# Layer 0 of a four-layer kernel, from units of 512 tokens to one pipeline of 128-token chunks

## The chip, the cores and the metric

The kernel runs on one core of a Trainium2 chip. A core has five engines with queues of their own: TensorE (PE in the profile, with its weight loads as PEld), VectorE (DVE), ScalarE (ACT), GpSimd (POOL) and SyncE (SP), which here issues the transfers. The metric is the device time of one execution in microseconds, and the time of a kernel is the median of its runs.

## The reference

The input x has 16 images of 192 channels and 32 x 32 pixels in float32. Four layers follow one another; only the first, an mLSTM block with a convolution, is touched. Ahead of it every image is group-normalised. Cut to what matters (S is 1024 tokens, INNER 384, 12 heads of 32):

```python
h = layernorm(seq)
x_in, z = split(h @ w_up + b_up)
x_act = silu(causal_conv4(x_in))
q, k, v = x_act @ w_q, x_act @ w_k, x_in
i_pre, f_pre = concat(q, k, v) @ w_i + b_i, concat(q, k, v) @ w_f + b_f
# scan over the tokens, for each head:
m_new = max(log_sigmoid(f) + m, i)
C_new = f_s * C + i_s * outer(v, k * 32 ** -0.5)
n_new = f_s * n + i_s * k * 32 ** -0.5
h = (C_new @ q) / max(abs(n_new @ q), 1)
# after the scan:
hn = (h - mean(h)) / sqrt(var(h) + 1e-5) * mh_w + mh_b      # per token and head
x1 = seq + ((hn + skip * x_act) * silu(z)) @ w_down + b_down
y = conv3x3(x1 + silu(seq @ w_lin + b_lin)) + conv2_b
y = leaky_relu(batchnorm(y))                                  # statistics over all images
```

Layers 1 to 3 (a Mamba block, a depthwise convolution with batch norm, a block with four scan directions) are the same in both kernels.

## The kernel before

Layer 0 works on 32 units, two for each image, of 512 tokens (U). Each unit has two parts, written as Python generators that yield between steps.

The front (`layer0_front`) loads and normalises the image (for the first unit of an image), applies the layer norm, the up projection (L452, evicted to xin at L454 and to sz at L456), the causal convolution on DVE (L460, L464), the x_lin projection (L472, L475), three silu passes on ACT (L479) between two loads of activation tables (the second is L481), q and k (L490, evicted at L494 and L496), and the gates. The gate part leaves three things: u and w, on 12 partitions, and a row in DRAM.

The back (`layer0_back`) turns the scan over tokens into four chunks of 128. `layer0_decays` transposes u and w. `layer0_weigh` reads the row back to all partitions as e (128 x 12 x 128), adds the causal mask (L576) and u (L577) on POOL and takes the exponential on ACT (L578). `layer0_chunk` does a chunk: scores of k and q (L654), transposes of k (L660, copied to kt at L661) and of xin (L664, copied to v at L667), p as scores times e on DVE (L671), the part from the carried state, it (L676), the part from the chunk, num (L681), their sum h, the division by the denominator (L693 to L696), and the new state (L702 to L713).

Once all four chunks stand in hs, the head norm takes the whole unit at once: mean (L601), subtraction (L603), square (L605), variance (L607), the power -0.5 on POOL (L610 takes its result; the power itself is recorded at the helper's line L240), then the transposes to channels first (L617), scale and bias on ACT (L621), skip on DVE (L624), gate on POOL (L625), and the down projection (L632, L635) into a padded image ypad. The 3 x 3 convolution of an image (`layer0_conv2`, L408, four parts of 18 matmuls) reads it once both of its units are there.

What sets the order: the program is traced in Python, and the framework's scheduler then lays each engine's queue out in the order in which, by its own times, instructions become ready, earlier traced ones first. At run time each queue goes in that order, with semaphore waits. The class `Side` spreads the front of unit i + 1 and the two convolution parts of the image before over the steps of unit i's back.

PSUM has eight banks here: two named mm, which take most results and the convolution's accumulation over half a unit, four for the scores (s), one for it and one for num. Most SBUF tiles have two buffers.

A float32 matmul shows as two records in the profile, a transpose as one.

Of the kernel before, what the change touches and what calls it, by code (L numbers as in the profile page):

```python
# [19 lines left out]
HP = 96  # L20
DI = 384
S = 1024
W = 32
# [172 lines left out]

class Unit:
# [8 lines left out]
class Program:  # L206
# [113 lines left out]
    def layer0(self):  # L320
        tc = self.tc
        with (
            tc.tile_pool(name="w0", bufs=1) as wp,
            tc.tile_pool(name="s0", bufs=2) as sp,
            tc.tile_pool(name="b0", bufs=2) as bp,
            tc.tile_pool(name="d0", bufs=3, space=DRAM) as dp,
            tc.tile_pool(name="ps0", bufs=2, space=PSUM) as psum,
        ):
            self.layer0_weights(wp, bp, psum)
            self.stats = wp.tile([HP, 2, 2 * self.nb, 6], F32, name="stats")  # L330
            n = self.nb * S // U
            self.unit = {}
            self.image = {}
            finish(self.layer0_front(0, sp, bp, dp, psum))
            side, yields = Side(), 20
            for i in range(n):
                b, u = divmod(i, S // U)
                if i + 1 < n:
                    side.add("front", self.layer0_front(i + 1, sp, bp, dp, psum), i, i + 0.95)
                if b > 0:  # L340
                    for j in range(2):
                        side.add("conv", self.layer0_conv2(b - 1, 2 * u + j, bp, psum), i + 0.5 * j, i + 0.5 * j + 0.5)
                done = 0
                for _ in self.layer0_back(i, sp, bp, psum):
                    done += 1
                    side.tick(i + min(done / yields, 1.0))
                yields = done
                side.tick(i + 1)
            for u in range(4):
                finish(self.layer0_conv2(self.nb - 1, u, bp, psum))  # L350
            self.batch_norm(sp, "0bn_g", "0bn_b", self.bn0)
# [47 lines left out]
    def layer0_conv2(self, b, part, bp, psum):  # L399
# [4 lines left out]
        ps = psum.tile([128, 512], F32, name="mm")  # L404
# [14 lines left out]
    def layer0_front(self, i, sp, bp, dp, psum):  # L419
# [64 lines left out]
        unit = {"xin": xin, "sz": sz, "xact": xact, "xl": xl}  # L484
        for w, name, scale in ((self.w_q, "q", 1.0), (self.w_k, "k", DH**-0.5)):
# [12 lines left out]
            if name == "q":  # L498
                yield from self.layer0_gates(unit, carry, sp, dp, psum)
        self.unit[i] = unit  # L500
# [70 lines left out]
    def layer0_weigh(self, c, unit, bp):  # L571

        nc = self.nc
        e = bp.tile([128, NH, 128], F32, name="e")
        nc.sync.dma_start(e, unit["row"][:, c * 128 : (c + 1) * 128].partition_broadcast(128))
        nc.gpsimd.tensor_tensor(e, e, self.k0("mask")[:, None, :].to_broadcast([128, NH, 128]), ADD)  # L576
        nc.gpsimd.tensor_tensor(e, e, unit["uw"][:, c, 0][:, :, None].to_broadcast([128, NH, 128]), ADD)  # L577
        nc.scalar.activation(e, e, AF.Exp)  # L578
        return e

    def layer0_back(self, i, sp, bp, psum):

        nc = self.nc
        b, u = divmod(i, S // U)
        unit = self.unit[i]
        xact, sz, xl = unit["xact"], unit["sz"], unit["xl"]
        state = None if u == 0 else self.unit.pop(i - 1)["state"]
        self.layer0_decays(unit, sp, psum)
        yield
        hs = bp.tile([128, NCH, NH, DH], F32, name="hs", bufs=1)  # L590
        e = [self.layer0_weigh(0, unit, bp)]
        for c in range(NCH):
            if c + 1 < NCH:
                e.append(self.layer0_weigh(c + 1, unit, bp))
            state = yield from self.layer0_chunk(u * NCH + c, c, unit, e[c], state, hs, sp, bp, psum)
        unit["state"] = state

        hv = hs.rearrange("p c h d -> p (c h) d")
        n = NCH * NH
        mean = sp.tile([128, n], F32, name="mhm")  # L600
        nc.vector.tensor_reduce(mean, hv, AX.X, ADD)  # L601
        nc.vector.tensor_scalar(mean, mean, 1.0 / DH, None, MUL)
        nc.gpsimd.tensor_tensor(hv, hv, mean[:, :, None].to_broadcast([128, n, DH]), SUB)  # L603
        sq = bp.tile([128, NH, 128], F32, name="e").rearrange("p h (c d) -> p (h c) d", d=DH)
        nc.scalar.activation(sq, hv, AF.Square)  # L605
        var = sp.tile([128, n], F32, name="mhv")
        nc.vector.tensor_reduce(var, sq, AX.X, ADD)  # L607
        nc.vector.tensor_scalar(var, var, 1.0 / DH, EPS, MUL, ADD)
        self.pow_mhalf(var)
        nc.gpsimd.tensor_tensor(hv, hv, var[:, :, None].to_broadcast([128, n, DH]), MUL)  # L610
        yield

        ht = bp.tile([128, 3, U], F32, name="ht", bufs=1)
        for t in range(3):
            ps = psum.tile([128, 512], F32, name="mm")
            for c in range(NCH):
                nc.tensor.transpose(  # L617
                    ps[:, c * 128 : (c + 1) * 128],
                    hs[:, c, 4 * t : 4 * t + 4].rearrange("p h d -> p (h d)"), self.k("ident"),
                )  # L620
            nc.scalar.activation(  # L621
                ht[:, t], ps, AF.Identity, bias=self.v128("0mh_b", t), scale=self.v128("0mh_w", t)
            )
            nc.vector.scalar_tensor_tensor(ht[:, t], xact[:, t], self.v128("0skip", t), ht[:, t], MUL, ADD)  # L624
            nc.gpsimd.tensor_tensor(ht[:, t], ht[:, t], sz[:, t], MUL)  # L625
            yield
        yp = self.ypad[b % 2]
        rows = U // W
        for m in range(2):
            ps = psum.tile([128, 512], F32, name="mm")  # L630
            for k in range(3):
                nc.tensor.matmul(  # L632
                    ps[:HP], self.w_down[:, k, m * HP : (m + 1) * HP], ht[:, k], start=k == 0, stop=k == 2
# [4 lines left out]
                xl[:, m].rearrange("p (a b) -> p a b", b=W), ADD, ADD,  # L638
            )
            yield  # L640

    def layer0_chunk(self, n, c, g, e, state, hs, sp, bp, psum):

        nc = self.nc
        q, k_, xin = g["q"], g["k"], g["xin"]
        ch = slice(c * 128, (c + 1) * 128)
        v1 = self.v1[n % 2]
        ev = e.rearrange("p (i j) t -> p j i t", j=4)

        ss = [psum.tile([128, 3, 128], F32, name="s", bufs=4) for _ in range(4)]  # L650
        for i in range(3):
            for j in range(4):
                part = slice(32 * j, 32 * j + 32)
                nc.tensor.matmul(ss[j][:, i], k_[part, i, ch], q[part, i, ch], start=True, stop=True)  # L654
        yield

        kt = bp.tile([128, DI], F32, name="kt")
        ps = psum.tile([128, 512], F32, name="mm")
        for t in range(3):
            nc.tensor.transpose(ps[:, t * 128 : (t + 1) * 128], k_[:, t, ch], self.k("ident"))  # L660
        nc.scalar.copy(kt, ps[:, :DI])  # L661
        ps = psum.tile([128, 512], F32, name="mm")
        for t in range(3):
            nc.tensor.transpose(  # L664
                ps[:, t * 128 : (t + 1) * 128], xin[:, t, 3 + c * 128 : 3 + (c + 1) * 128], self.k("ident")
            )
        nc.scalar.copy(v1[:, :, :DH], ps[:, :DI].rearrange("p (h d) -> p h d", h=NH))  # L667
        p = []
        for j in range(4):
            p.append(bp.tile([128, 3, 128], F32, name="p", bufs=3))  # L670
            nc.vector.tensor_tensor(p[j], ss[j], ev[:, j], MUL)  # L671
        yield
        if state is not None:
            it = psum.tile([128, 512], F32, name="it", bufs=1)
            for i in range(3):
                nc.tensor.matmul(it[:, i * 132 : (i + 1) * 132], q[:, i, ch], state[:, i], start=True, stop=True)  # L676
        yield
        num = psum.tile([128, NH, DH + 1], F32, name="num", bufs=1)
        for j in range(4):
            for i in range(3):  # L680
                nc.tensor.matmul(num[:, 4 * i + j], p[j][:, i], v1[:, 4 * i + j], start=True, stop=True)  # L681
        yield
        h = bp.tile([128, NH, DH + 1], F32, name="h")
        if state is None:
            nc.vector.tensor_copy(h, num)
        else:
            nc.vector.tensor_tensor(
                h, it[:, :396].rearrange("p (h d) -> p h d", h=NH),
                g["uw"][:, c, 1][:, :, None].to_broadcast([128, NH, DH + 1]), MUL,
            )  # L690
            nc.vector.tensor_tensor(h, h, num, ADD)
        den = sp.tile([128, NH], F32, name="den")
        nc.vector.scalar_tensor_tensor(den, h[:, :, DH], -1.0, h[:, :, DH], MUL, MAX)  # L693
        nc.vector.tensor_scalar(den, den, 1.0, None, MAX)
        nc.vector.reciprocal(den, den)  # L695
        nc.gpsimd.tensor_tensor(hs[:, c], h[:, :, :DH], den[:, :, None].to_broadcast([128, NH, DH]), MUL)  # L696

        vr = bp.tile([128, NH, DH + 1], F32, name="vr")
        nc.gpsimd.tensor_tensor(vr, v1, e[:, :, 127][:, :, None].to_broadcast([128, NH, DH + 1]), MUL)  # L699
# [780 lines left out]
```

## Time and profile before

The kernel takes 19,994.89 us, the median of three runs from 19,978.39 to 20,020.1. The profiled execution has a span of 20,007.8 us.

| engine | busy, us | share of the span | share from 80 to 4740 us |
|---|---|---|---|
| PE | 17,439.3 | 87% | 3,628.10 of 4,660 (78%) |
| DVE | 13,103.0 | 65% | 1,817.57 (39%) |
| ACT | 12,711.5 | 64% | 1,084.05 (23%) |
| POOL | 12,611.8 | 63% | 1,695.59 (36%) |

The last column is layer 0's stretch. The page's second part cuts the span into 40 slices of about 500 us and gives the busy share of each in tenths; the row PEclk gives the TensorE clock that was granted, in tenths of full speed. A group of instructions is listed with its line, engine, operation, the tiles it writes and reads, its count, its busy time and the mean of one, and the idle time of the engine before it with what ended it. Line numbers are those of the kernel before.

### The profile page before, as it was taken

The page shows a single profiled execution, that of the slowest core. Times are in us where ns is not written, and L with a number is a line of the kernel's source. Part 1 is how long each engine was busy: PE and PEld are TensorE (multiplying, and loading weights), DVE is VectorE, ACT ScalarE, POOL GpSimd, SP SyncE. Part 2 cuts the span into 40 slices and gives each one's busy share as a digit, 9 for nine tenths or more (in the row PEclk, how much of TensorE's full clock was granted, in tenths as well). Part 3 has the DMA queues.
Part 4 walks back from the last instruction along what each step waited for, and adds up shares of the span by engine and source line. Part 5 has one row for each costly group of instructions (what it writes and reads, how often), then busy time and mean ns, then how long its engine had stood idle before and what let it go on. Part 6 is the DMA issues. An engine that isn't in the chain of part 4 may idle for free. (4 is left out here: it accounts for less than half of the span.)

```text
span 20007.8 us, 251373 instructions
## 1 busy us (share of the span) xinstructions
PE 17439.3 (87%) x92796; PEld 11473.9 (57%) x92796; DVE 13103.0 (65%) x14590; ACT 12711.5 (64%) x21185; POOL 12611.8 (63%) x6105
## 2 busy tenths in 40 slices
PE   7777777777999999978899999989998999999898
PEld 3343334434555555546666666666666666666666
DVE  3333343333777777747677877777787778777778
ACT  2222222223666666638778887888788788878888
POOL 3333333333555555537677877787787778877878
PEclk8888888888999999989999999999999999999999
DMA  1111111111222222212222222222222222222222
GB/s 40 25 27 30 27 27 29 26 26 39 62 60 61 61 61 61 60 59 64 74 70 77 75 74 71 77 72 74 73 77 73 70 77 77 73 71 77 72 72 65
DMA packets 713002, 1194.70 MB, mean 60 GB/s; under 512 B 60733, under 2 KB 300062, under 8 KB 699390
## 3 DMA queue, kind: packets, MB, share of 16 engines
q1 hardware_dynamic: 711774, 1178.62, 20.0%
q8 instruction: 735, 12.04, 0.2%
q14 instruction: 493, 4.04, 0.1%
HBM read 1030.13 MB, written 148.25 MB: 59 GB/s over the span
## 5 line engine op out<-in xcount | busy, mean ns | idle before, releaser
L847 POOL TENSOR_TENSOR h<-h,cb 128x1536 f32<-128x1536 f32 x2560 | 8848.5, 3460 | 1207.3 <-DVE h L840 1033.3
L821 ACT ACTIVATE da<-dt,neg_a 128x512 f32<-128x512 f32 x7680 | 5170.6, 714 | 1575.9 <-DVE h L840 1503.7
L828 PE MATMUL xb<-const,xbt 128*128 128x128 f32 x30720 | 5139.3, 283 | 506.4 <-ACT xbt L812 249.7
L840 DVE TENSOR_TENSOR_SCAN h<-da,carry,xb 128x512 f32<-128x512 f32 x3840 | 4663.4, 1263 | 1202.8 <-PE xb L828 923.4
L812 ACT ACTIVATE xbt<-ut,bt 128x384 f32<-128x384 f32 x8960 | 4880.2, 605 | 579.7 <-PE xb L828 572.0
L840 DVE TENSOR_TENSOR_SCAN h<-da,xb 128x512 f32<-128x512 f32 x3840 | 4442.0, 1202 | 1147.0 <-PE xb L828 851.3
L828 PEld LDWEIGHTS xb<-const,xbt 128*128 128x128 f32 x30720 | 3782.9, 145 | 2121.7 <-issue 866.1
L858 PE MATMUL y<-const,h 128*128 128x128 f32 x30720 | 4796.9, 280 | 66.5 <-POOL h L847 33.7
L858 PEld LDWEIGHTS y<-const,h 128*128 128x128 f32 x30720 | 3737.7, 145 | 231.6 <-issue 68.3
L810 POOL TENSOR_SCALAR xbt<-ut,bt 128x384 f32<-128x384 f32 x1280 | 1595.9, 1247 | 1476.4 <-PE xb L828 1074.8
L1401 PE MATMUL mm<-xin,dconv 128*128 128x512 f32 x3072 | 1461.3, 620 | 188.7 <-DMA dconv<-d_conv 187.6
L408 PE MATMUL mm<-ypad,w_conv 96*96 96x512 f32 x2304 | 1196.4, 638 | 11.8 <-ACT kt L661 6.3
L846 POOL COPY carry<-h 128x3 f32<-128x3 f32 x1280 | 245.9, 192 | 1424.0 <-DVE h L840 1321.6
L1401 PEld LDWEIGHTS mm<-xin,dconv 128*128 128x128 f32 x3072 | 576.7, 197 | 831.6 <-issue 632.4
L696 POOL TENSOR_TENSOR hs<-h,den 128x384 f32<-128x384 f32 x128 | 107.5, 840 | 1108.4 <-DVE den L695 1108.4
L578 ACT ACTIVATE e<-e 128x1536 f32<-128x1536 f32 x128 | 189.8, 1483 | 931.4 <-POOL e L577 913.0
L738 PE MATMUL mm<-xc,w_x 128*44 128x512 f32 x960 | 654.3, 800 | 54.9 <-ACT xc L1072 54.5
L757 PE MATMUL mm<-dbl,w_dt 65*128 65x512 f32 x960 | 525.6, 633 | 119.7 <-DVE dt L762 86.3
L408 PEld LDWEIGHTS mm<-ypad,w_conv 96*96 96x96 f32 x2304 | 370.4, 175 | 439.2 <-issue 412.1
L699 POOL TENSOR_TENSOR vr<-v,e 128x396 f32<-128x396 f32 x128 | 122.9, 960 | 791.6 <-ACT v L667 791.6
L1163 PE MATMUL mm<-xpad,d_dw 96*96 96x512 f32 x1152 | 587.5, 649 | 38.6 <-DVE xpad L1143 38.6
L1163 PE MATMUL mm<-xpad,dconv 96*96 96x512 f32 x1152 | 569.3, 633 | 54.9 <-DMA dconv<-d_dw 41.6
(272 smaller groups left out, 18918.4 us busy)
## 6 DMA issues: line engine op xcount, KB each, us to landing
cb<-row SPq DMA_DIRECT2D x2560, 256.0 KB
e<-row SPq DMA_DIRECT2D x128, 768.0 KB
dconv<-d_conv SPq DMA_DIRECT2D x144, 512.0 KB
x<-x SPq DMA_DIRECT2D x48, 768.0 KB
sz<-tmp SPq DMA_DIRECT2D x32, 768.0 KB
xrows<-xtok SPq DMA_DIRECT2D x32, 768.0 KB
xtok<-xrows SPq DMA_DIRECT2D x128, 192.0 KB
tmp<-sz SPq DMA_DIRECT2D x32, 768.0 KB
```

Source lines behind the costliest of these rows:

```text
L408: nc.tensor.matmul(ps[:HP], self.w_c2[:, k, t, m * HP : (m + 1) * HP], yp[:, k, r0 : r0 + 16, t % 3 : t % 3 + W], start=t + k == 0, stop=t ...
L738: nc.tensor.matmul(ps[:XD], w_x[t], seen[:, t], start=t == 0, stop=t == 2)
L757: nc.tensor.matmul(ps, w_dt[:, t * 128 : (t + 1) * 128], dbl, start=True, stop=True)
L810: nc.gpsimd.tensor_scalar(t[:, c], u.ut[:, c], b, None, MUL)
L812: nc.scalar.activation(t[:, c], u.ut[:, c], AF.Copy, scale=b)
L821: nc.scalar.activation(da[i, t], u.dt[:, t], AF.Exp, scale=u.neg_a(t, n))
L828: in_order(nc.tensor.transpose(xb[i, t][:, c * 128 : (c + 1) * 128], xbt[i][:, c, t * 128 : (t + 1) * 128], ident))
L840: nc.vector.tensor_tensor_scan(hv, dv, xv, 0.0 if first else u.carry_in[:, n, t : t + 1], MUL, ADD)
L847: nc.gpsimd.tensor_tensor(h[i], h[i], u.c.pop(n)[:, None, :].to_broadcast([128, 3, 512]), MUL)
L858: in_order(nc.tensor.matmul(u.y[:, j], h[i][:, t, c * 128 : (c + 1) * 128], ident, is_transpose=True, start=n == 0 and j % 4 == 0, stop=n ...
L1163: self.nc.tensor.matmul(ps, diags[t], pad[:, r0 : r0 + 16, c0 : c0 + W], start=t == 0, stop=t == n - 1)
L1401: nc.tensor.matmul(ps, dc[:, j], xin[:, r0 : r0 + 16, j % 4 : j % 4 + W], start=n == 0 and j == 0, stop=n == 1 and j == 7,)
```

## The change

In the changed kernel layer 0 has no backs. One loop goes over all 128 chunks of all images (`for g in range(n + 2)`), and each step does parts of four chunks: the down projection of chunk g - 2 if it is the last of its unit, p, h and the state of chunk g, weights and scores of chunk g + 1, the transposes, gate and skip of chunk g - 1, and the head norm of chunk g. Fronts and convolution parts are spread over the steps by fixed times. The purpose is that the chain of norm, gate and down projection never stands between two units with nothing beside it.

The norm is now per chunk, without the division: with d = max(n q, 1 in absolute value), (h/d - mean) / sqrt(var + eps) is (h - mean h) / sqrt(var h + eps d^2), where h is undivided. The power -0.5 is exp(-0.5 ln(.)) on ACT. Bias, skip, weight and gate are folded at the end of the front: xs = (skip x_act + mh_b) silu(z) and sw = mh_w silu(z), so that a chunk needs one product and one sum. kt is copied on DVE instead of ACT. The convolution accumulates in a PSUM bank of its own, and it goes to the mm pair.

```diff
+            for i in range(1, self.nb * S // U):
+                side.add("front", self.layer0_front(i, sp, bp, dp, psum), NCH * i - 3.9, NCH * i - 1.2)
+            for b in range(self.nb - 1):
+                for j in range(4):
+                    at = 8 * b + 9.2 + 1.9 * j
+                    side.add("conv", self.layer0_conv2(b, j, bp, psum), at, at + 1.9)
...
+            for g in range(n + 2):
+                for j, _ in enumerate(self.layer0_step(g, n, chunks, sp, bp, psum)):
+                    side.tick(g + j / 8)
...
-        ps = psum.tile([128, 512], F32, name="mm")
+        ps = psum.tile([128, 512], F32, name="conv", bufs=1)
...
+        for t in range(3):
+            nc.scalar.activation(
+                xact[:, t], xact[:, t], AF.Identity, bias=self.v128("0mh_b", t), scale=self.v128("0skip", t)
+            )
+        nc.gpsimd.tensor_tensor(xact, xact, sz, MUL)
+        yield
+        for t in range(3):
+            nc.scalar.activation(sz[:, t], sz[:, t], AF.Copy, scale=self.v128("0mh_w", t))
+        unit |= {"xs": xact, "sw": sz}
...
-        nc.scalar.copy(kt, ps[:, :DI])
+        nc.vector.tensor_copy(k.kt, ps[:, :DI])
...
-            it = psum.tile([128, 512], F32, name="it", bufs=1)
+                it = psum.tile([128, 512], F32, name="mm")
...
+    def layer0_step(self, g, n, chunks, sp, bp, psum):
+        k, new = chunks.get(g), None
+        last = chunks.pop(g - 2, None)
+        if last and last.c == NCH - 1:
+            self.layer0_down(last.unit, psum)
+        yield
+        if k:
...
+            yield
...
+            yield
+            self.layer0_state(k, vr, chunks.get(g - 1) if g % (S // 128) else None, bp, psum)
+            yield
+        if new:
+            yield from self.layer0_scores(new, bp, psum)
+        if g - 1 in chunks:
+            self.layer0_output(chunks[g - 1], bp, psum)
+            yield
+        if k:
+            self.layer0_norm(k, h, sp, bp)
+            yield
...
+    def layer0_norm(self, k, h, sp, bp):
+        nc.vector.tensor_reduce(mean, x, AX.X, ADD)
+        nc.vector.tensor_scalar(mean, mean, 1.0 / DH, None, MUL)
+        nc.gpsimd.tensor_tensor(hs, x, mean[:, :, None].to_broadcast([128, NH, DH]), SUB)
+        nc.scalar.activation(sq, hs, AF.Square)
+        nc.vector.tensor_tensor(d, h[:, :, DH], h[:, :, DH], MUL)
+        nc.vector.tensor_scalar(d, d, 1.0, EPS, MAX, MUL)
+        nc.vector.tensor_reduce(var, sq, AX.X, ADD)
+        nc.vector.scalar_tensor_tensor(var, var, 1.0 / DH, d, MUL, ADD)
+        nc.scalar.activation(var, var, AF.Ln)
+        nc.scalar.activation(var, var, AF.Exp, scale=-0.5)
+        nc.gpsimd.tensor_tensor(hs, hs, var[:, :, None].to_broadcast([128, NH, DH]), MUL)
+
+    def layer0_output(self, k, bp, psum):
...
+        nc.vector.tensor_tensor(
+            ht, k.unit["sw"][:, :, k.tok], ps[:, :DI].rearrange("p (t n) -> p t n", t=3), MUL
+        )
+        nc.gpsimd.tensor_tensor(ht, ht, k.unit["xs"][:, :, k.tok], ADD)
```

Not shown, and new only in place: `layer0_state`, `layer0_scores` and `layer0_down` hold the lines that `layer0_chunk` and `layer0_back` had. In the changed kernel's numbering p is L638, vr L640, it L652, num L664, the state L687 to L698, the norm L708 to L722, the head transposes L732, the product and sum of the output L735 and L738, the convolution L416.

## The prediction

> **What bounds the kernel now.** The page's slices come first. The change touches layer 0 alone, and the slices show where that layer lies: the first nine or so of forty, with TensorE (PE) at seven tenths and its clock row at eight.
>
> ```profile
> PE   7777777777999999978899999989998999999898
> POOL 3333333333555555537677877787787778877878
> PEclk8888888888999999989999999999999999999999
> ```
>
> Then the stretch from 80 to 4740 us, which holds the 32 units of layer 0, and the mark of one instruction that stands once in each unit:
>
> ```profile
> 80.00:4740.00 4660.00, 3628.10 (x14552) 1870.58 (x14552) 1817.57 (x3150) 1084.05 (x1349) 1695.59 (x780) 0.84 0.11 27
> L610 POOL TENSOR_TENSOR hs<-hs,mhv x32: 2772/2774/2782, 209.8 to 4725.4; 128x1536 f32<-128x1536 f32 x32
> ```
>
> The columns of the first line are length, busy time of PE, weight load, DVE, ACT and POOL, then clock and DMA. PE is busy 78% and nothing else above 39%; DMA is at 0.11. A unit takes (4725.4 - 209.8) / 31 = 145.7 us. PE idles (4660 - 3628) / 32 = 32.2 us of it. The list of what PE waited for, on the tiles named mm, says where (us, times):
>
> ```profile
>   POOL hs L610: 526.1, 32
>   ACT q L494: 116.9, 16
>   ACT xin L454: 83.1, 15
>   ACT xl L475: 67.4, 15
>   ACT sz L456: 66.7, 28
> ```
>
> Half, 16.4 us per unit, is one wait: the transposes of the normed heads (L617) for L610. The next four are evictions by ACT, 10.4 us per unit. The timeline of POOL at the end of one unit shows the first:
>
> ```profile
> 4301.51 2.78 POOL L603 TENSOR_TENSOR hs<-hs,mhm 128x1536 f32<-128x1536 f32 x1 [2.15 <-DVE mhm L602]
> 4308.36 8.02 POOL L240 TENSOR_TENSOR mhv<-mhv,const 128x48 f32<-128x48 f32 x1 [4.07 <-DVE mhv L608]
> 4316.34 3.42 POOL L576 TENSOR_TENSOR e<-e,const 128x1536 f32<-128x1536 f32 x1
> 4319.71 2.78 POOL L610 TENSOR_TENSOR hs<-hs,mhv 128x1536 f32<-128x1536 f32 x1
> ```
>
> An 8.02 us power on 48 columns, a mask addition of the next unit that stands ahead, then the product. PE has nothing else in its queue meanwhile. What that does to the clock:
>
> ```profile
> 4270.00:4305.00 35.00, 34.93 (x156) 18.21 (x155) 17.76 (x37) 4.92 (x8) 5.41 (x5) 1.00 0.13 24
> 4309.00:4323.00 14.00, 1.02 (x7) 0.75 (x7) 0.69 (x1) 0.68 (x1) 14.00 (x4) 0.62 0.25 67
> 4323.00:4345.00 22.00, 16.89 (x70) 8.37 (x69) 10.56 (x14) 5.30 (x5) 13.64 (x7) 0.81 0.00 1
> ```
>
> The dense stretch ahead runs at 1.00, the gap falls to 0.62, and the 22 us after it stand at 0.81. So an idle microsecond is paid twice.
>
> **What the skill says.** The Trainium skill, "TensorE: Matmul & The Clock Gate", Part 1, says the PE clock falls to half after an idle window of about 3.4 us and returns after as long a busy one; the three lines agree. "GPSIMD Engine Reference", 4.1 Engine selection, counts GpSimd about 2x slower than VectorE on two-input elementwise work and keeps it off PSUM; here a 128x396 product takes 0.94 us on POOL (L699) against 0.57 us on DVE (L691). "ScalarE: Activation LUTs", Table sets, has ln and exp in one set, natural_log_exp_and_others; the set is already loaded at L481, and each load here takes 1.283 us. "PSUM — Partial Sum Buffer", Engine vs sequencer instructions, calls the ScalarE, VectorE and GpSimd queues strict FIFO; this is what makes L610 wait behind L576 above, and it is the danger of the new norm.
>
> **PE's work, which stays.** Both kernels have the same matmuls. At full clock the 144 records of the last convolution give the price of a 512-column record:
>
> ```profile
> 4739.15 61.98 PE L408 MATMUL mm<-ypad,w_conv 96*96 96x512 f32 x144
> ```
>
> 61.98 / 144 = 0.430 us. A unit has 72 such records of convolution, 24 of up projection, 18 + 18 of q and k, 12 of gates, 12 of down, 8 of w_lin, 8 of layer norm: 172 x 0.430 = 74.0 us. A chunk's small matmuls, from start to next start in the dense stretch: num 2.5, state 0.76, scores 0.88, the transposes of k, v and heads 0.33 each, it 0.67, together 5.8 us, times 4 is 23.2. Decays and group norm add about 1.3 (an estimate from 14 records of some 0.1). Sum: 98.5 us. So of today's 145.7 us, 32.2 are idle and 145.7 - 32.2 - 98.5 = 15.0 are PE running on a lowered clock, 0.47 us for each idle one.
>
> **The change, part by part.**
> - Norm per chunk, one chunk late. It removes the unit-end chain and its 16.4 us wait: the power (8.0 us of POOL), two 128x1536 products and two 1.75 us reductions go. Each chunk gets two POOL operations of 0.83 us (size of L696), a square on ACT (about 0.48, size of L667), two reductions on DVE (1.75 / 4 = 0.44, with overhead 0.5), five small DVE operations of 0.2, Ln and Exp on 12 columns (about 0.2 to 0.3). As a chain: 0.7 on DVE, 0.83 POOL, 0.48 ACT, 0.7 DVE, 0.5 ACT, 0.83 POOL, some 4.0 us, plus up to 6.2 if it falls behind both additions to e (3.43 + 2.75) on POOL. Its consumer, the head transposes, comes a chunk of some 29 us later. Hidden, unless the in-order queues stop something else: the reduction of the squares (L718) waits on DVE for POOL and ACT, and behind it stand the products p of the next chunk, for which num on PE waits. Bounds per chunk: 0 (PE has convolution and front in its queue) and 6. I take 1.5, so 6 per unit.
> - Own bank for the convolution, and "it" moves into the mm pair. Today the convolution holds one of two mm banks over half a unit and all others share one; the 10.4 us of eviction waits are partly this. Afterwards two banks serve all but the convolution, with the 3 "it" matmuls as new guests. Bounds: all 15.8 us of non-L610 idle remain, or 5. I take 8.
> - Gate and skip folded ahead: three ACT passes of about 0.68 for xs and three for sw, one POOL product of 128x1536 (2.8 to 3.4), against three ACT (0.78), three DVE (1.88) and three POOL (1.56) passes of 128x512 removed. kt moves from ACT to DVE (0.48 us to about 0.57). Sums per unit: POOL 53 to about 45, DVE 57 to about 57, ACT 34 to about 35. None comes near 100 us: nothing on the path, by PE's own work beside it.
> - Stray table loads: 92 loads stand in layer 0's ACT queue before, 64 after; 28 x 1.28 = 36 us of ACT in all, hidden, taken as zero.
> - Down projection two chunks late, pipeline fill and drain: fill and drain lengthen by a chunk's latency, about 10 us, and lose the last 15.6 us wait. With one bank the four last convolutions each wait for an eviction (0.7 us and hops): 4 us. Together taken as +4.
> - Layers 1 to 3: the same instructions in the same order, from 4810 us on; zero.
>
> Sum for a unit: 98.5 + 14 idle (6 + 8) + 14 x 0.47 = 6.6 is 119.1 us. Saved: (145.7 - 119.1) x 32 = 851, less 4, so 19,995 - 847 = 19,148, called **19,150 us**.
>
> **The rivals.**
> - A: as above, with idle between 8 and 20 us per unit. Chance 0.59.
> - B: nearly dense, 5 us idle a unit; the stretch from 4270 to 4305 us, with 35.00 - 34.93 = 0.07 us idle over more than a chunk, shows that chunks can run so. Then 98.5 + 5 + 2.4 = 105.9 us, 39.8 x 32 = 1,274 saved: 18,720. Against it, the evictions still share ACT with 6.5 us bursts of silu and table loads. Chance 0.13.
> - C: the wait moves rather than goes. Four small norms a unit hold up DVE, ACT and POOL in order, and idle stays at 26: 98.5 + 26 + 12.2 = 136.7, 9.0 x 32 = 288 saved: 19,710. For it: waits of 5 to 16 us by in-order POOL and ACT are everywhere in the list of waits. Chance 0.17.
> - D: slower. The norm's chain stands in every chunk's path: 6 us x 4 on top of the 15.8 left makes 40 idle, 98.5 + 40 + 18.8 = 157.3, 11.6 x 32 = 371 lost: 20,370. Against it: the chain of about 10 us at worst is well within a chunk of 29. Chance 0.09, and 0.02 for a result inside 0.2%.
>
> **How the numbers follow.** The time is A's, the likeliest. The range starts at B's value, which leaves out the lower half of B (0.06), and ends at 19,870, where 28 us of idle (139.7 us a unit, 19,803) meet 67 us for a worse fill and drain: above it lie the last of C (0.03), no change (0.02) and D (0.09). That leaves out 0.2. Faster is A, B and C, 0.89; same 0.02; slower D, 0.09.
>
> **What would show it.** Right: in layer 0 PE at about 88% or more and clock above 0.92; no single wait near 526 us; the interval of a unit near 119 us; waits of PE on evictions below 10 us per unit; the sum from 4810 us on unchanged at 15,197. Step of the norm wrong: waits of DVE for ACT sq and of PE num for DVE p of more than 3 us per chunk. Step of the banks wrong: PE still waiting for ACT xin, sz, q and xl some 10 us per unit. Step of the clock wrong: idle gone but the clock still near 0.84. The forecast would fail altogether if in-order stalls of PE came to over 30 us per unit.

## The result

The changed kernel takes 19,377.4 us (median of four runs, 19,358.88 to 19,390.29) against 19,989.36 us before (four runs): a ratio of 0.9691, 95% interval 0.9674 to 0.9708. It saves 612 us where 847 were forecast; the time lies in the range.

The page of the changed kernel, its rows for TensorE, POOL and the granted clock:

```profile
PE   8899898989999999789989999998998999899898
POOL 3333333336555555547787788778778878877878
PEclk8988888989999999899999999999999999999999
```

Layer 0 ends one slice earlier. PE is at eight to nine tenths there, but its clock row has hardly moved from eight. Two stretches, of length, busy time of PE, weight load, DVE, ACT and POOL, clock and DMA share: layer 0 without its last convolutions, and all that follows it.

```profile
80.00:4100.00 4020.00, 3614.48 (x14530) 1878.62 (x14529) 1971.73 (x3563) 1112.37 (x1640) 1442.38 (x876) 0.88 0.13 32
4170.00:19363.00 15193.00, 13688.39 (x77991) 9540.94 (x77989) 11264.58 (x11394) 11605.78 (x19811) 10908.35 (x5314) 0.95 0.24 70
```

Layers 1 to 3 take 15,193 us against 15,197: no change. In layer 0 PE is busy 90% instead of 78%. The list of what PE waited for on mm tiles (us, times) has lost its head:

```profile
  ACT v L621: 84.7, 22
  DVE kt L613: 77.4, 30
  DVE x L439: 43.1, 23
  ACT xl L483: 42.8, 13
  ACT xin L462: 33.4, 27
  ACT lnsq L319: 31.1, 13
  DVE k L504: 27.4, 14
```

The 526.1 us behind L610 have no counterpart. From here on a unit is measured between the first and the last of the 32 copies uw (one in each unit), and all kernels are laid side by side by it. The mark and the stretch between the two marks, of the kernel before and of the changed one:

```profile
L567 DVE COPY uw<-mm x32: 256/257/258, 98.3 to 4634.6; 128x96 f32<-128x96 f32 x32
98.30:4634.60 4536.30, 3532.34 (x14155) 1816.46 (x14156) 1774.20 (x3071) 1066.37 (x1326) 1653.27 (x760) 0.84 0.11 28
L585 DVE COPY uw<-mm x32: 256/258/258, 96.3 to 4001.6; 128x96 f32<-128x96 f32 x32
96.30:4001.60 3905.30, 3507.79 (x14037) 1818.25 (x14031) 1921.93 (x3455) 1093.39 (x1607) 1401.24 (x849) 0.88 0.13 32
```

In the changed kernel 3905.3 / 31 = 126.0 us for a unit, of which (3905.30 - 3507.79) / 31 = 12.8 are idle. The prediction's sum put PE's work at full clock at 98.5; the rest, 126.0 - 12.8 - 98.5 = 14.7, is put down to PE working on a lowered clock and called the clock loss below. By the same marks the kernel before has 146.3 = 98.5 + 32.4 idle + 15.4 clock loss. So idle fell by 19.6 us a unit, where 18.2 were forecast, and the clock loss, which was to fall to 6.6, hardly moved.

The clock loss is a remainder and takes in any error of the 98.5. The trace also has a record of the granted clock, which is 1 or 0.5 throughout. Half of the time that PE is busy at 0.5 comes to 12.6 us a unit before and 13.4 after. So remainders can be off by some 3 us, and differences of 1 or 2 us between them mean little; that the clock loss did not fall holds either way.

### The profile page after: what moved, and what is told of

Same layout as the page of the kernel before. It is cut to its first block, busy times and chain, and to the rows that moved or that the text cites. A ratio compares the mean times of both kernels' runs of the same rounds, so it can differ in the third digit from the quotient of the medians.

```text
span 19362.9 us, 252255 instructions
## 1 busy us (share of the span) xinstructions
PE 17417.7 (90%) x92796; PEld 11470.4 (59%) x92796; DVE 13260.0 (68%) x15006; ACT 12740.5 (66%) x21477; POOL 12359.0 (64%) x6201
## 4 chain that ended last, share of the span: by engine, by line
PE 27%; ACT 11%; DVE 6%; issue 5%; POOL 5%; DMA 3%; SPq 0%; POOLq 0%; DVEq 0%; ACTq 0%
PE mm L1440 7%; PE xb L867 6%; PE y L897 6%; ACT xbt L851 4%; ACT da L860 4%; DVE h L879 4%; POOL h L886 4%; DMA dconv<-d_conv 2%; PE mm L1202 2%; PE mm L777 2%; PE mm L796 1%; POOL xbt L849 1%; PE mm L1421 1%; PE mm L1476 1%; PE mm L817 1%
## 5 line engine op out<-in xcount | busy, mean ns | idle before, releaser
L416 PE MATMUL conv<-ypad,w_conv 96*96 96x512 f32 x2304 | 1244.5, 660 | 3.1 <-ACT y L423 3.1
L711 POOL TENSOR_TENSOR hs<-h,mhm 128x384 f32<-128x384 f32 x128 | 106.4, 831 | 1019.0 <-DVE den L716 894.0
L594 POOL TENSOR_TENSOR e<-e,const 128x1536 f32<-128x1536 f32 x128 | 444.8, 3475 | 429.7 <-DMA e<-row 377.6
L416 PEld LDWEIGHTS conv<-ypad,w_conv 96*96 96x96 f32 x2304 | 377.4, 179 | 443.4 <-issue 424.4
L1202 PE MATMUL mm<-xpad,d_dw 96*96 96x512 f32 x1152 | 589.9, 651 | 37.5 <-DVE xpad L1182 37.5
```

Source lines behind the costliest of these rows:

```text
L416: nc.tensor.matmul(ps[:HP], self.w_c2[:, k, t, m * HP : (m + 1) * HP], yp[:, k, r0 : r0 + 16, t % 3 : t % 3 + W], start=t + k == 0, stop=t ...
L1202: self.nc.tensor.matmul(ps, diags[t], pad[:, r0 : r0 + 16, c0 : c0 + W], start=t == 0, stop=t == n - 1)
```

## The experiments

All measured with their own runs of the kernel before beside them; the ratio is to those.

| kernel | ratio to before (95%) | unit, us | idle | clock loss |
|---|---|---|---|---|
| before | 1 | 146.3 | 32.4 | 15.4 |
| bank_alone | 0.9918 (0.9903 to 0.9933) | 141.4 | 25.6 | 17.3 |
| lnexp_alone | 0.9871 (0.9854 to 0.9888) | 137.8 | 24.1 | 15.3 |
| conv_in_mm | 0.9800 (0.9779 to 0.9821) | 132.3 | 18.1 | 15.7 |
| no_lag | 0.9692 (0.9677 to 0.9707) | 125.4 | 12.5 | 14.4 |
| the change | 0.9691 (0.9674 to 0.9708) | 126.0 | 12.8 | 14.7 |
| gather3 | 0.9658 (0.9639 to 0.9678) | 123.3 | 9.4 | 15.4 |
| kt_on_act | 0.9628 (0.9612 to 0.9644) | 122.1 | 9.7 | 14.0 |
| three_banks | 0.9564 (0.9546 to 0.9581) | 117.4 | 7.6 | 11.3 |
| three_banks_squares | 0.9538 (0.9524 to 0.9552) | 116.3 | 8.3 | 9.5 |
| three_banks_kt | 0.9536 (0.9520 to 0.9552) | 116.4 | 7.4 | 10.4 |
| three_banks_gather3 | 0.9533 (0.9519 to 0.9548) | 116.2 | 6.6 | 11.1 |
| all_together | 0.9528 (0.9512 to 0.9544) | 116.1 | 6.0 | 11.6 |

### What the parts are worth

**lnexp_alone**, the kernel before without the power on POOL:

```diff
         nc.vector.tensor_scalar(var, var, 1.0 / DH, EPS, MUL, ADD)
-        self.pow_mhalf(var)
+        nc.scalar.activation(var, var, AF.Ln)
+        nc.scalar.activation(var, var, AF.Exp, scale=-0.5)
```

> The kernel before with one edit: the power -0.5 of the head norm as Ln and Exp on ACT, whose table set is loaded, instead of 8.02 us on POOL. Theory (the power is half of the 16.4 us wait of the head transposes): the wait falls to about 8 us, and since a wait of 8 us still drops the clock the cold loss stays at 15 us per unit: 19,989 - 256 = about 19,735 us. Rival (the mask addition and other POOL work take its place): the wait stays over 13 us, 19,900 us or more.

Measured 19,721.76 us. The wait of the head transposes (the product is L611 here) is 237.6 / 32 = 7.4 us per unit instead of 16.4, in PE's list for the mm tiles:

```profile
  POOL hs L611: 237.6, 32
  ACT q L494: 113.9, 16
```

The theory holds, in both of its halves: the power was over half of the wait, and with 8.3 us less idle per unit the clock loss stays (15.3; 12.3 by the clock's record, 12.6 before). This one edit, without any pipeline, brings 1.29% of the change's 3.09%.

**bank_alone** and **conv_in_mm**, the convolution's bank put into the kernel before, and taken out of the changed one:

```diff
-        ps = psum.tile([128, 512], F32, name="mm")
+        ps = psum.tile([128, 512], F32, name="conv", bufs=1)
...
-            it = psum.tile([128, 512], F32, name="it", bufs=1)
+            it = psum.tile([128, 512], F32, name="mm")
```

> The kernel before with one part of the change: the convolution in its own bank, it in the mm pair. Theory (the bank is worth by itself what undoing it cost in the changed kernel, 198 us, since the eviction waits of 10 us per unit are there before as well): about 19,790 us. Rival (without the pipeline the units' own chain sets the time and the waits are made up): 19,930 us or more.

> The changed kernel with the bank undone: the convolution accumulates in an mm bank again and it has a bank of its own. Theory (the own bank is worth the 8 us per unit that the prediction gave it): eviction idle returns, idle about 20 us per unit, about 19,650 us. Rival (the chunk pipeline alone took the wait away): within 60 us of 19,377.

Measured 19,838.89 us and 19,575.39 us. The bank alone gains 0.82%; undone in the changed kernel, it costs 198 us and leaves 18.1 us of idle. Both theories hold in kind, and both sizes were put some 35 to 75 us too high. The bank's value is much the same with and without the pipeline, 0.82 and 1.1%. With the 1.29% of the power this would leave 0.7 to 1% of the 3.09% for everything else, the pipeline included. That is only an estimate: no run has the power and the bank together without the pipeline, and none has the pipeline with the power still on POOL, so that they add up isn't shown, and the pipeline's own worth isn't either.

**no_lag**, the changed kernel with a chunk's transposes and gate right after its own norm:

```diff
-        if g - 1 in chunks:
-            self.layer0_output(chunks[g - 1], bp, psum)
-            yield
         if k:
             self.layer0_norm(k, h, sp, bp)
             yield
+            self.layer0_output(k, bp, psum)
+            yield
```

> The changed kernel with the transposes, gate and skip of a chunk traced right after its own norm instead of one chunk later. Theory (the lag is what hides the norm's chain of some 5 us): PE waits for hs in most of the 128 chunks, 3 to 5 us each with a lowered clock after some, about 19,377 + 500 = 19,900 us. Rival (the scheduler lets later matmuls pass, so the lag in the program text buys little): within 100 us of 19,377.

Measured 19,386.92 us: the rival. PE's waits for the normed heads appear (L721 is the norm's last product here), but with 52 us in all they are 1.6 a unit:

```profile
  DVE kt L613: 74.6, 38
  ACT lnsq L319: 63.4, 23
  POOL hs L721: 52.0, 21
```

Which chunk's output stands in the step is not what hides the norm. A likely reason is that the scheduler lets the next chunk's and the convolution's matmuls pass in any case, and that the chunk pipeline has such matmuls there at every norm; no run takes those away.

### Banks

**three_banks**, num into the mm tiles, which become three:

```diff
-            tc.tile_pool(name="ps0", bufs=2, space=PSUM) as psum,
+            tc.tile_pool(name="ps0", bufs=3, space=PSUM) as psum,
...
-            num = psum.tile([128, NH, DH + 1], F32, name="num", bufs=1)
+            num = psum.tile([128, 512], F32, name="mm")[:, : NH * (DH + 1)].rearrange("p (h d) -> p h d", h=NH)
```

> The changed kernel with num taken into the mm banks, which are three instead of two. Theory (PE's remaining 12.7 us of idle per unit are waits for a free mm bank): idle falls to about 6 us per unit and some low-clock stretches with it, 19,377 - 215 - 60 = about 19,100 us. Rival (the evicting engine is late in its own queue, and another bank only moves the wait): idle 11 us or more, 19,320 us or more.

Measured 19,104.7 us, as the theory said. PE's list for its mm tiles:

```profile
  ACT lnsq L319: 71.8, 31
  ACT q L502: 34.3, 13
  DVE kt L613: 32.6, 16
  DVE k L504: 22.8, 14
  ACT v L621: 17.6, 7
```

v falls from 84.7 to 17.6 us, kt from 77.4 to 32.6. The engines that copy were not too slow; there was no bank to go on with. num also leaves its single bank here, but in the changed kernel PE never waited for that bank: its waits before num are for p (7.7 us in all) and v (6.5). The first entry is not a bank but a data dependence of the layer norm.

**kt_on_act**, the changed kernel with the copy of kt on ACT again:

```diff
-        nc.vector.tensor_copy(k.kt, ps[:, :DI])
+        nc.scalar.copy(k.kt, ps[:, :DI])
```

> The changed kernel with one of its parts undone: kt is copied on ACT again instead of DVE. Theory (the head transposes wait some 4 us at the start of each unit for the mm bank that kt holds, because DVE has a 9 us run of the causal convolution ahead, and each such wait drops the clock for some 20 us): the wait of L732 for kt goes, about 70 us of idle and half of 16 x 20 us of half clock, 19,377 - 230 = about 19,150 us. Rival (ACT has runs as long, the silu block, and the same wait comes back there): within 60 us of 19,377.

Measured 19,252.06 us, 125 us less than the change, between the two. The time is nearer to the theory, but the wait that was to go did not go. The wait on kt is there as before, on the other engine (66.6 us of it at the head transposes, 70.7 in the change); what went are the waits on v:

```profile
  ACT lnsq L319: 89.1, 34
  ACT kt L613: 81.5, 34
  ACT xl L483: 45.5, 14
```

So this part of the change cost about 0.6%, against 3.09% gained in all. Why it shows as waits on v (84.7 us to none), xin (33.4 to 6.2) and x (43.1 to 22.2), and not on kt, was not looked for. Why kt is late on DVE is seen in the timeline of the changed kernel (start, length, engine):

```profile
1169.05 3.43 POOL L513 TENSOR_TENSOR xact<-xact,sz 128x1536 f32<-128x1536 f32 x1 [0.35 <-ACT xact L510]
1170.00 2.50 DVE L719 SCALAR_TENSOR_TENSOR mhv<-mhv,den 128x12 f32<-128x12 f32 x1
1172.43 3.45 POOL L594 TENSOR_TENSOR e<-e,const 128x1536 f32<-128x1536 f32 x1
1173.02 4.73 DVE L698 SCALAR_TENSOR_TENSOR state<-state,dec 128x132 f32<-128x132 f32 x3
1178.60 0.54 DVE L613 COPY kt<-mm 128x384 f32<-128x384 f32 x1
1179.20 0.90 PE L732 MATMUL mm<-const,hs 128*128 128x128 f32 x3 [3.56 <-DVE kt L613]
L719 DVE SCALAR_TENSOR_TENSOR mhv<-mhv,den x128: 155/171/2795, 133.0 to 4094.3; 128x12 f32<-128x12 f32 x128
```

(The last line gives the count of L719 and its shortest, median and longest time in ns.) Twelve columns take DVE 2.50 us, until POOL's folded gate (L513) ends. The three state updates take 4.73 us: the first, 3.02 us long, ends 0.16 us after POOL's mask addition, the others behind the next two POOL instructions. Their medians are 0.17 and 0.35 us each. The Trainium skill, "SBUF — State Buffer", Who interferes with whom, says that a DVE instruction with two SBUF inputs contends with a GpSimd one that reads SBUF, and the trace agrees: the 45 L719 that start while a 128x1536 instruction runs on POOL all end 0.03 us after it, with a mean of 1.96 us, and the other 83 take 0.17. Stretched instructions like these stand between the transposes of k and the copy in 19 of the 25 waits of L732 for kt that are over 0.3 us, so the causal convolution that the expectation named is not the cause. It is a new wait between norm and DVE, as the prediction feared, but it comes from POOL and shows on PE as a bank that is not free. With kt on ACT the stretched instructions are still there, and cost less.

**three_banks_kt**, both:

> Three mm banks and kt copied on ACT, together. Theory (kt on DVE hurt only because a late copy held one of two mm banks, so with three its place does not matter): within 60 us of three_banks alone, 19,105. Rival (the late copy is a wait of its own): the 125 us that kt on ACT saved with two banks are saved again, about 18,990 us.

Measured 19,066.41 us: 38 us below three_banks, inside the theory's 60. With a third bank the place of the copy matters little.

### The clock

**gap_alone** puts the price of a gap by itself. The segments, cut:

```python
for n in (1, 3, 5, 8, 24):
    for mixed in (0, 1):
        s = self.segment(s, w, n, mixed, bp, psum)
...
    nc.scalar.activation(t[:HP], ps[:HP], AF.Identity, scale=0.01)
    for _ in range(n - 1):
        nc.scalar.activation(t[:HP], t[:HP], AF.Identity, scale=0.9)
```

> Leaves out the whole computation: 60 segments of 512-column matmuls on TensorE alone, with idle gaps of about 1, 2, 3.5, 5.5 and 16 us made by a chain of ACT passes, each gap followed by 60 wide matmuls or by a mixture of small and wide ones as in the chunks (five times 12 of 33 columns, 3 of 132, 2 of 512) and then 60 wide. Theory (the clock's price is paid by the gap, not by its length, and the mixture prolongs it): gaps of 5.5 and 16 us are followed by the same low stretch, some 5 us before wide matmuls and 20 us or more before the mixture; gaps of 1 us by none. Rival (price in proportion to the gap, 0.47 us per idle us): the 16 us gap costs three times the 5.5 us one, and what follows makes no difference.

The time that the granted clock then stayed at half, from the end of a gap to the next gap, by the clock's record in the trace (five or six of each kind; least and most):

| gap, us | low after it, wide matmuls follow | low after it, the mixture follows |
|---|---|---|
| 0.74 | 0 | 0 or 37.5 |
| 2.16 | 3.4 to 6.8 | 23.9 to 30.7 |
| 3.48 | 3.4 to 6.3 | 9.7 to 10.2 |
| 5.46 | 5.1 to 6.9 | 27.9 to 37.7 |
| 16.04 | 4.1 to 6.6 | 9.9 to 27.9 |

(Left out are the last of the mixed 16 us gaps, which no gap follows, and the first mixed gap of the run, which was 2.03 us instead of 0.74 and had 37.5 us after it.) Three stretches of it: wide matmuls after 16 us of idle, the mixture after 16 us, and the mixture after 0.74 us. The columns are length, PE, weight load, ACT, POOL, clock, DMA.

```profile
1553.60:1557.60 4.00, 3.95 (x5) 1.53 (x6) 0.00 (x0) 0.00 (x0) 0.50 0.00 0
1557.60:1567.60 10.00, 10.00 (x24) 3.75 (x23) 0.00 (x0) 0.00 (x0) 0.99 0.00 0
2202.40:2209.40 7.00, 7.00 (x31) 6.76 (x32) 0.00 (x0) 0.00 (x0) 0.50 0.00 0
2209.40:2219.40 10.00, 10.00 (x35) 7.63 (x34) 0.00 (x0) 0.00 (x0) 0.50 0.00 0
839.20:876.70 37.50, 37.50 (x144) 29.17 (x144) 0.00 (x0) 0.00 (x0) 0.54 0.00 0
```

The core of the theory holds, not all its figures. From 2.16 us on, a gap of 16 us costs no more clock than a small one. What follows decides: under wide matmuls the clock is back in 3.4 to 6.9 us; under the mixture PE is busy without a pause for the 17 us shown and the clock stays at half, and in the 37.5 us shown it is at half for 34. But the mixture was not always followed by 20 us or more (9.7 at the least), and gaps of 0.74 us were followed by a low clock before the mixture, three times of five, though theory said none. The clock's record has one thing more: inside the mixture the clock falls 12 times, for 3.4 us each, with no gap before it at all, and under wide matmuls never. So a gap isn't needed; after the 0.74 us gaps too it falls only 2.1 us into the mixture. The times with the mixture alternate from repetition to repetition, and why was not looked for. Nor was what it is in the mixture that matters: its matmuls are narrower, but weight loads also fill 6.76 of 7.00 us there against 1.53 of 4.00 under wide ones, and no run parts the two.

In the changed kernel itself the wait of L732 above is such a case; the stretches ahead of it, with it, and after it (columns as in the result, with DVE):

```profile
1168.00:1174.00 6.00, 6.00 (x46) 3.44 (x45) 5.21 (x5) 2.77 (x7) 5.65 (x3) 1.00 0.31 61
1174.00:1178.00 4.00, 1.63 (x4) 0.32 (x2) 4.00 (x4) 1.19 (x3) 3.60 (x4) 0.91 0.00 0
1178.00:1202.00 24.00, 22.80 (x89) 15.08 (x89) 8.20 (x21) 2.69 (x3) 6.45 (x4) 0.50 0.18 41
1202.00:1214.00 12.00, 12.00 (x56) 6.74 (x51) 5.14 (x8) 2.27 (x4) 6.88 (x5) 0.89 0.01 1
```

A gap of 3.56 us is followed by 24 us at 0.50, with PE 95% busy. Its work there, on the timeline, is two convolution matmuls at a time between decays, it, num, state and scores:

```profile
1185.66 1.69 PE L652 MATMUL mm<-state,q 128*128 128x132 f32 x6
1187.14 3.62 PE L416 MATMUL conv<-ypad,w_conv 96*96 96x512 f32 x4
1190.56 3.89 PE L664 MATMUL num<-v,p 128*128 128x33 f32 x18
1194.26 1.23 PE L687 MATMUL mm<-vr,kt 128*128 128x132 f32 x4
```

num takes 3.89 us, against 2.09 for the same 18 records at clock 1.00. Counted by the clock's record between the marks, the kernel before has 118 falls of the clock, the changed one 80; but in the kernel before the 16.5 us gap before L617 was followed by 7.2 us of half clock on average, and in the changed one the small gaps before L732 (3.8 us, 16 times) and L652 (3.4 us, 17 times) by 20.0 and 14.1 us.

**gather3** tries on the kernel whether wide matmuls in longer runs bring the clock back. In the changed kernel:

```diff
                     start=t + k == 0, stop=t + k == 9,
                 )
-            yield
+            if t % 3 == 2:
+                yield
```

> The changed kernel with the convolution handed out in pieces of six matmuls instead of two; nothing else differs. Theory (the clock comes back only after some 3.4 us filled with wide matmuls, and the changed kernel's thin mixture of small and wide ones starves it): the 14.8 us per unit that PE loses to the half clock fall to about 10, layer 0's mean clock rises from 0.88 to about 0.91, idle stays near 12.7 us per unit, 19,377 - 150 = about 19,230 us. Rival (the clock follows the share of idle alone): clock 0.88, time within 40 us of 19,377.

Measured 19,299.81 us, 78 us less, but not as the theory said. The clock loss did not fall (15.4), and idle did, from 12.8 to 9.4. The low stretches did become shorter, from a mean of 11.8 to 10.2 us, but there are 94 falls instead of 80, 14 of them at a 0.8 us gap before the group norm's second matmul and 15 with no gap over 0.3 us in the 5 us before them (2 such in the change). The rival, a clock that follows idle alone, fits no better: the time is 78 us off where it allowed 40. So gathering is not a cure in itself. It also leaves longer stretches of small matmuls alone: in 8 of those 15 the 3.5 us ahead hold no 512-column matmul.

**three_banks_gather3**, gathering on top of the third bank:

> Three mm banks and the convolution in pieces of six matmuls. Theory (gathered wide matmuls let the clock return sooner after each gap): the low stretches, 13 us each with three banks, shorten to about 10, some 3 us x 1.9 per unit x 32 / 2 = 90 us, about 19,010 us. Rival (pieces of six keep the chunk's own matmuls waiting, and new gaps give it back, as in gather3, where there were more drops of the clock): 19,105 us or more.

Measured 19,065.48 us, 39 us below three_banks, where 90 were expected: again through idle (6.6), with the clock loss at 11.1. The low stretches did shorten as the theory said, from 12.9 to 9.2 us, but there are 77 of them instead of 60.

**three_banks_squares**, against the layer norm's wait: a second buffer for the squares, in layer 0 alone (on top of the third bank):

```diff
-            sq = pool.tile([128, 512], F32, name="lnsq", bufs=1)
+            sq = pool.tile([128, 512], F32, name="lnsq", bufs=2 if n == U and p == HP and len(xs) == 2 and pool is getattr(self, "bp0", None) else 1)
...
+            self.bp0 = bp
```

> Three mm banks and two buffers instead of one for the squares of layer 0's layer norm. Theory (of the gaps left with three banks, the one ahead of the variance matmuls, 21 of 60 drops of the clock and 72 us of idle, is the second square waiting for the first one's matmul): about half of it goes, 19,105 - 36 - 70 = about 19,000 us. Rival (the wait is for the first square and for ACT's queue): within 40 us of 19,105.

Measured 19,078.61 us, 26 us less: the rival's side. Idle did not fall (8.3); the clock loss did, to 9.5.

**all_together**:

> Three mm banks, kt on ACT, pieces of six convolution matmuls and two buffers for the squares. Theory (what is left are separate small gaps, so the three savings of about 40, 40 and 26 us add up): 19,105 - 106 = about 19,000 us. Rival (each of them moves the same stretch of half clock about, which is there once): about 19,060 us, as with any one of them.

Measured 19,071.1 us. This is the rival's number: any one of the three on top of the third bank gives what all of them give, within the intervals. The rival's reason is not shown, though the record fits it: 79 falls of the clock instead of three_banks' 60, 23 of them with no gap over 0.3 us in the 5 us before. These versions, at 0.953 to 0.954, beat the kernel before by 4.6 to 4.7% and the change by 1.6%; which of them is best is not settled, and their intervals overlap with that of three_banks alone (0.9546 to 0.9581).

## Why the prediction was right, and where it was off

The direction, the range and the main mechanism were right: the 16.4 us wait went, and the likeliest case A came, with idle of 12.8 us per unit within its 8 to 20. PE busy 90%, eviction waits under 10 us and unchanged later layers came as its signs said; the clock of layer 0, at 0.88, lies between the 0.92 named for right and the 0.84 for wrong. By steps:

- PE's work, 98.5 us, the same matmuls: the sum closes by definition, since the clock loss is what is left. With the clock's record in its place, 98.5 + 32.4 + 12.6 and 98.5 + 12.8 + 13.4 miss the measured units by 2.8 and 1.3 us, so 98.5 is somewhat low.
- Norm per chunk, 6 us of idle per unit taken: too much.

```profile
PE num L664 <- DVE p L638: 7.7, 2, 7.2
DVE mhv L718 <- ACT sq L713: 143.5, 99, 4.4
```

(us in all, times, longest.) PE waited 7.7 us for p, 6.5 for v at num, 2.0 for p at the scores and 0.2 for the normed heads in all of layer 0, 0.5 a unit. DVE's wait for the squares is there (143.5 us in 99 times), but PE hardly waits behind it. That the lag in the program hides it was the wrong reason, as no_lag shows.
- Banks, 8 us taken: the waits on evictions (v, kt, xl, xin, k, ypad 10.6 and q 9.6) make 285.9 us, 8.9 a unit. As evictions right in size, and three_banks shows the cause. But the term stood for all idle outside the norm, and that is 12.8 - 0.5 = 12.3: waits for x (43.1 us in all) and for the squares of the layer norm (31.1), among others, were left out. So the 14 us of idle came out near 12.8 with some luck, by a norm term 5.5 too high and a bank term 4.3 too low.
- The clock, "14 x 0.47 = 6.6": this is the term that was mis-sized, and it makes nearly all of the miss. It measured 14.7, 8.1 a unit more; over 32 units 259 us, less 38 for the idle that was 1.2 below the 14 taken, is 221 of the 227 us between 19,150 and 19,377. (By the clock's record it is 13.4, 6.8 more, or 218 us.) The step that failed is "an idle microsecond is paid twice". The loss had been divided by the idle time and made a rate. It does not go with the length of a gap; how long the clock stays low depends on the matmuls that follow, and in part it falls without a gap. The 16.4 us wait, once a unit, was cheap for each idle microsecond: taking it off took much idle and hardly any clock loss, which lnexp_alone shows in the small. The prediction's own lines held this: of the 22 us at 0.81, 8.3 were at half clock, but only the first 3.0 followed from the long gap; the rest are two new falls, at 4329.4 and 4343.1 us. The prediction had the Trainium skill's sentence ("TensorE: Matmul & The Clock Gate", Part 1) that a busy window of about 3.4 us brings the clock back. gap_alone agrees for wide matmuls (3.4 to 6.9 us of half clock) and does not for the mixture (9.7 to 37.7).
- Gate folding and kt on DVE, "nothing on the path": kt_on_act shows 125 us for kt. The sums came as forecast for POOL (45.2 us a unit) and ACT (35.3); DVE has 62.0 instead of 57, since its instructions are stretched beside POOL's. The step looked at engine totals and not at which copies hold an mm bank and what stands ahead of them. Within the total this is part of the bank waits and of their clock loss.
- Layers 1 to 3, zero: 15,193 us against 15,197.
- The sign of a wrong norm step, waits of num for p of over 3 us a chunk, did not come (7.7 us in all). B's 5 us of idle were nearly reached with a third bank (6.0 in all_together), but with a clock loss of 11.6 a unit takes 116.1 us there and not 105.9.

Why mixed work doesn't bring the clock back, and wide matmuls do, stays open. That it is so is shown for matmuls alone, in gap_alone. In the kernel it is read from the traces, and the two runs that gathered the wide matmuls made the low stretches shorter and more frequent, without a clear fall of the clock loss. Whether the clock loss of a unit can be brought far below 10 us was not tried beyond these versions.

## What to carry to other kernels

Where the granted clock drops, count its falls, and look at the gaps before them and at what runs after them; a long gap before wide matmuls can cost less clock than a short one in the middle of small ones, so a loss per idle microsecond taken from one kernel doesn't hold for its successor. Give an accumulation that lasts long its own PSUM bank, and then look whether the short-lived tiles have enough: here a third bank brought 1.3%, beside 3.1% for the whole change. Before a chain is restructured, take its one dear instruction out alone: the power was 1.29 of 3.09%.

## What the runs showed of the hardware

- With a mixture of 33-, 132- and 512-column float32 matmuls after a gap of only 0.74 us, the TensorE clock was at half for 34 of 37.5 us in which PE was busy without a pause (three of five times); after the same gap and wide matmuls it never fell (six times). Inside the mixture it also fell 12 times with no gap before it.
- A DVE instruction on 12 columns with two SBUF inputs took up to 2.795 us, with a median of 0.171, when a 128 x 1536 instruction ran on POOL, whose end it waited for in 45 of 45 cases; in the changed kernel this is 102.2 us of L719's busy time over layer 0.
- A power on 128 x 48 took 8.02 us on POOL; Ln and Exp on 128 x 12 take 0.21 us each on ACT.
